# AdaLN modulation with a two-expert FFN on one core: the first unit of z with its fifth product moved forward

## The chip, the cores and the metric

The kernel runs on one core of one Trainium2 chip. The metric is the device time of one execution in microseconds, as the median of several runs. The kernel before took 1694.98 us (three runs, 1694.61 to 1696.77).

## What is computed

Cut to what matters, with x of shape (2, 2048, 512), one condition vector per batch, and all in float32:

```python
ys = y / sqrt(512)
d  = rsqrt((ys*ys) @ (weight*weight) + 1e-8)
z  = ((x * ys[:, None, :]) @ weight) * d[:, None, :]      # 4096 tokens, 512 wide
e  = argmax(softmax(z @ gate_w.T))                        # one of two experts
routed: every expert sees z where the token is its own, and zeros otherwise
        sum over experts of relu(masked @ w1[e] + b1[e]) @ w2[e] + b2[e]
shared: relu(z @ sw1 + sb1) @ sw2 + sb2
out = x + routed + shared
```

The expert that a token is not routed to sees a zero row, so that it adds a constant, `relu(b1) @ w2 + b2`.

## The kernel before, in words

The program has three parts. The first computes z from xT and the modulated weight `cws = cw * ys` (512 x 512, one for each batch), in four units of 1024 tokens, `z_unit(u)`. The second is the shared FFN over the same four units, and the third the routed FFN over tokens that are sorted by expert. Almost all of the time is in the second and third; the change touches the first unit of the first part and what is loaded for it.

Every large product is written as a 2 x 2 block product with seven block products in place of eight (Winograd's form). In `z_unit`, `a11, a12, a21, a22` are 256 x 256 blocks of `cws` (a11 and a12 are the left half of the output columns, for the low and the high rows; a21 and a22 the right half), and `x11, x12, x21, x22` are 256 x 512 blocks of xT (x11 low rows and first 512 tokens, x12 low rows and last 512, x21 and x22 the high rows). The sums of weights are `s1 = a21 + a22`, `s2 = s1 - a11`, `s3 = a11 - a21`, `s4 = a12 - s2`, and those of tokens are `x1 = x12 - x11`, `x2 = x22 - x1`, `x12 = x22 - x12` (in place) and `x4 = x21 - x2`, all on VectorE. The products are 1: a11 x11; 2: a12 x21, added onto product 1; 5: s1 x1; 6: s2 x2; 7: s3 x12; 4: a22 x4; 3: s4 x22, added onto product 5. Each is four 128 x 128 by 128 x 512 float32 matmuls, which the profile shows as eight passes (line 444).

Product 1 stays in PSUM until ScalarE has copied it (`c1`, line 459), since product 2 is added onto it. `u2 = p6 + c1` and `u3 = p7 + u2` are on VectorE (lines 469 and 476). The order on TensorE in the first unit is 1, 2, pd, 6, pv, 7, pb, 5, 4, 3. Here pd, pv and pb are the parts of a generator, `modulation_parts` (lines 229 to 261): pd multiplies `ys2 = ys * ys` by the squares of cw, which ScalarE makes; pv turns the result onto partitions, from which VectorE and ScalarE make `dd`; pb makes the bias row. `scaled` multiplies a part of z by `dd` on ScalarE (line 454). In the later units the parts of the generator are absent, and transposes of the unit before (`rows_of`, line 395) stand between the products; each is copied by ScalarE into one of four buffers with the tag `io`, scored on VectorE and stored by GpSimd.

Every engine takes its instructions in the order of the code, and a wait holds all that stands behind it on the same engine. VectorE's order in the first unit is: the four products of `modulate` for the left half, the four for the right half, the four sums of weights, ys2, rb1 (`relu(b1)`), then x1, x2, x12, x4.

PSUM has two rings of four banks, `pa` and `po`. pd, pv and pb take banks of `po`, and so do products 1 and 5; products 6, 7 and 4 take `pa`.

Transfers have three queues, issued by SyncE (SP), ScalarE (ACT) and GpSimd (POOL). The first loads are:

| Queue | Order before |
|---|---|
| SP | cond, cw left half rows 0, rows 1, rows 2 and 3 (line 146), cw right half (148), x22 (150), x for unit 1, gate |
| ACT | x11 in two parts, x21 (147), x12 (149), b1, b2 |
| POOL | 512 KB of zero rows written to zD and accD (180, 181) |

"Rows k" are the 128 rows k of cw, one k to a step of a matmul's sum. The zero rows are read much later, by gathers of padding tokens; their source is a buffer of the tag `io`, set to zero by VectorE (line 179). The transfers on SP and ACT share eight semaphores in turn, so that the ninth waits for the first to land, and so on.

Of the kernel before, what the change touches and what calls it, by code (L numbers as in the profile page):

```python
# [9 lines left out]
F32 = mybir.dt.float32  # L10
# [6 lines left out]
def kernel(  # L17
# [52 lines left out]
    U = 2 * T  # L70
# [17 lines left out]
    const = ctx.enter_context(tc.tile_pool(name="const", bufs=1))  # L88
    wpool = ctx.enter_context(tc.tile_pool(name="wpool", bufs=3))
# [18 lines left out]
    zD = dram.tile([N + P, D], F32, name="zD")  # L108
    zTD = [dram.tile([P, KD, U], F32, name=f"zTD{u}") for u in range(NU)]
    accD = dram.tile([N + P, D], F32, name="accD")  # L110
# [33 lines left out]
        nc.sync.dma_start(cw_sb[:, k, :half], cw_v[:, k, :half])  # L144
        nc.scalar.dma_start(xt[0][:, k, :T], xT_v[:, k, :T])
    nc.sync.dma_start(cw_sb[:, K2:, :half], cw_v[:, K2:, :half])
    nc.scalar.dma_start(xt[0][:, K2:, :T], xT_v[:, K2:, :T])
    nc.sync.dma_start(cw_sb[:, :, half:], cw_v[:, :, half:])
    nc.scalar.dma_start(xt[0][:, :K2, T:], xT_v[:, :K2, T:U])
    nc.sync.dma_start(xt[0][:, K2:, T:], xT_v[:, K2:, T:U])  # L150
    b1_sb = const.tile([P, E + 1, HC], F32, name="b1_sb")
    nc.scalar.dma_start(b1_sb, b1T.rearrange("e p c -> p e c"))
    b2_sb = wpool.tile([P, D], F32, tag="w1", name="b2_sb")
# [21 lines left out]
        out=before, in_=before, compare_op=ALU.is_ge, fill=1.0,  # L175
        base=0, pattern=[[-1, P]], channel_multiplier=1,
    )
    zero_rows = io("zero_rows")
    nc.vector.memset(zero_rows, 0.0)
    nc.gpsimd.dma_start(zD[N:, :], zero_rows)  # L180
    nc.gpsimd.dma_start(accD[N:, :], zero_rows)
    tok_i = const.tile([P, NB], I32, name="tok_i")
    nc.gpsimd.iota(tok_i, pattern=[[P, NB]], base=0, channel_multiplier=1)
    tok_f = const.tile([P, NB], F32, name="tok_f")
# [17 lines left out]

    ys = const.tile([P, KD, B], F32, name="ys")
    nc.vector.tensor_scalar_mul(ys, cond_sb, SCALE)
    cws = work.tile([P, B, KD, D], F32, tag="O", name="cws")

    def modulate(b, parts=(slice(0, D),)):
        for part in parts:
            for k in range(KD):
                nc.vector.tensor_scalar_mul(cws[:, b, k, part], cw_sb[:, k, part], ys[:, k, b : b + 1])  # L210
# [5 lines left out]
    def sums0(b, tile):  # L216

        sums([tile[:, i] for i in range(4)], *halves(cws[:, b]))
        return tile

    modulate(0, (slice(0, half), slice(half, D)))
    cwS = {0: sums0(0, wpool.tile([P, 4, K2, K2 * P], F32, tag="w2", name="cwS0"))}
    ys2 = const.tile([P, KD, B], F32, name="ys2")
    nc.vector.tensor_mul(ys2, ys, ys)
    cw2 = wpool.tile([P, KD, D], F32, tag="w2", name="cw2")
    dd = const.tile([P, KD, B], F32, name="dd")
    bsum = const.tile([P, KD], F32, name="bsum")
# [1 line left out]
    def modulation_parts():  # L229
        for k in range(KD):  # L230
            nc.scalar.activation(cw2[:, k, :], cw_sb[:, k, :], AF.Square)
        var = const.tile([P, KD, B], F32, name="var")
        pd = bank("po", "pd")
        for k in range(KD):
            nc.tensor.matmul(pd[:B, :D], ys2[:, k, :], cw2[:, k, :], start=(k == 0), stop=(k == KD - 1))
        vr = work.tile([P, D], F32, tag="zrow", name="vr", bufs=2)
        nc.vector.tensor_scalar_add(vr[:B, :], pd[:B, :D], EPS)
        yield
        pv = bank("po", "pv")
        for o in range(KD):  # L240
            nc.tensor.transpose(pv[:, ts(o, B)], vr[:B, ts(o, P)], ident[:B, :B])
        nc.vector.tensor_copy(var.rearrange("p k b -> p (k b)"), pv[:, : KD * B])

        root = const.tile([P, KD, B], F32, name="root")
        nc.scalar.activation(root, var, AF.Sqrt)
        d0 = const.tile([P, KD, B], F32, name="d0")
        nc.vector.reciprocal(d0, root)
        nt = const.tile([P, KD, B], F32, name="nt")
        nc.vector.tensor_mul(nt, d0, d0)
        nc.vector.tensor_mul(nt, nt, var)  # L250
        nc.vector.tensor_scalar(nt, nt, -0.5, 1.5, ALU.mult, add)
        nc.vector.tensor_mul(dd, d0, nt)
        yield

        pb = bank("po", "pb")
        for o in range(KD):
            nc.tensor.matmul(
                pb[:, o : o + 1], b2_sb[: E + 1, ts(o, P)], ones[: E + 1, :1], start=True, stop=True
            )
        nc.vector.tensor_copy(bsum, pb[:, :KD])  # L260
        yield
# [64 lines left out]

    part = {}
    rb1 = const.tile([P, E, HC], F32, name="rb1")
    nc.vector.tensor_scalar_max(rb1, b1_sb[:, :E, :], 0.0)

    zero_late = []

# [89 lines left out]
    def z_unit(u):  # L422

        b = u * U // (N // B)
        x_ = xt[u]
        z_ = zt[u] = work.tile([P, KD, U], F32, tag=f"h{2 + u % 2}", name=f"zt{u}")
        rows = list(range(U // P)) if u > 0 else []
        a11, a12, a21, a22 = halves(cws[:, b])
        s1, s2, s3, s4 = (cwS[b][:, i] for i in range(4))
        x11, x12, x21, x22 = x_[:, lo, t0], x_[:, lo, t1], x_[:, hi, t0], x_[:, hi, t1]  # L430
        x1, x2, x4 = (
            work.tile([P, K2, T], F32, tag=tag, name=f"x{i}_{u}", bufs=2)
            for i, tag in ((1, "cr"), (2, "cr"), (4, "cs"))
        )

        def product(tag, j, a, x, ps=None):
            start = ps is None
            if rows:
                rows_of(u - 1, rows.pop(0), "po" if j in (6, 7, 4, 3) else "pa")
            if start:  # L440
                ps = [bank(tag, f"z{j}_{u}_{i}") for i in range(K2)]
            for k in range(K2):
                for i in range(K2):
                    nc.tensor.matmul(
                        ps[i], a[:, k, ts(i, P)], x[:, k, :],
                        start=(start and k == 0), stop=(k == K2 - 1), skip_group_check=not start,
                    )
# [12 lines left out]
        nc.vector.tensor_sub(x1, x12, x11)  # L460
        nc.vector.tensor_sub(x2, x22, x1)
        nc.vector.tensor_sub(x12, x22, x12)
        nc.vector.tensor_sub(x4, x21, x2)
        product("po", 2, a12, x21, p1)
        if u == 0:
            next(modulation)
        p6 = product("pa", 6, s2, x2)
        for i in range(K2):
            nc.vector.tensor_add(u2[i], p6[i], c1[i])
        if u == 0:  # L470
            next(modulation)
        for i in range(K2):
            scaled(z_[:, i, t0], p1[i], i)
        p7 = product("pa", 7, s3, x12)
        for i in range(K2):
            nc.vector.tensor_add(u3[i], p7[i], u2[i])
        if u == 0:
            next(modulation)
        if u == NU - 1:
            z_sums()  # L480
            first[0][1]()
        p5 = product("po", 5, s1, x1)
        for i in range(K2):
            nc.vector.tensor_add(z_[:, K2 + i, t1], p5[i], u3[i])
            scaled(z_[:, K2 + i, t1], z_[:, K2 + i, t1], K2 + i)
        if u == 0:
            modulate(1)
        if u == NU - 1:
            first[1][1]()
        if u == 1:  # L490
            cwS[1] = sums0(1, wpool.tile([P, 4, K2, K2 * P], F32, tag="w2", name="cwS1"))
        p4 = product("pa", 4, a22, x4)
        for i in range(K2):
            nc.vector.tensor_add(z_[:, K2 + i, t0], p4[i], u3[i])
            scaled(z_[:, K2 + i, t0], z_[:, K2 + i, t0], K2 + i)
# [27 lines left out]
    for u in range(NU):  # L523
        if u == NU - 1:
            first += [made(c) for c in range(2)]
        z_unit(u)
        if u + 2 < NU:
            load_xT(u + 2)
        if u == 0:
            nc.vector.tensor_sub(gdiff, gate_sb[:, 1, :], gate_sb[:, 0, :])  # L530
        if u == 1:
            load_z(0)

# [835 lines left out]
```

## Time and profile before

| What | Value |
|---|---|
| Median of three runs | 1694.98 us (1694.61 to 1696.77) |
| The profiled execution | 1696.22 us, with a span of 1694.5 us |
| TensorE busy | 1678.6 us, 99% of the span |
| VectorE busy | 1071.9 us, 63% |
| ScalarE, GpSimd busy | 335.5 us and 221.8 us |
| Mean granted TensorE clock | 0.998 |
| DMA | 335.30 MB, a mean of 198 GB/s |
| First product starts | 6.17 us |
| First product of unit 1 starts | 42.38 us |

The span runs from the first to the last instruction of the profiled execution; its time includes what lies around them. PE is TensorE's matmuls, DVE is VectorE, ACT is ScalarE, SP is SyncE. In a timeline a line gives start, duration, engine, line of the kernel, operation, result and operands by the program's names, and in brackets how long the engine had been idle before it and what released it. In a table of stretches each engine has its busy time and its number of instructions, and the last three columns are the granted clock of TensorE, the DMA engines' busy share and GB/s.

### The profile page before, as it was taken

Reading aid. Unit: us, or ns where it says so; the run is one execution under the profiler, and the core shown is the slowest. Engines: PE = TensorE matmul, PEld = TensorE weight load, DVE = VectorE, ACT = ScalarE, POOL = GpSimd, SP = SyncE. Lnnn points to the kernel's source line nnn. Section 1 sums busy time; section 2 is a strip of 40 time slices with the busy share of each in tenths; the row PEclk is TensorE's granted clock in tenths of the full one; section 3 lists DMA queues with packets and bytes.
Section 4 is the critical chain, followed back from the end, with each engine's and each line's share of the span. In section 5 each row is a group of like instructions: output and inputs, shape, how many; then the busy total and the mean of one; then the engine's idle time right before and its main releaser. Section 6 shows DMA issues by size and latency. Waiting matters only on the chain. (4 is left out here: it accounts for less than half of the span.)

```text
span 1694.5 us, 18012 instructions
## 1 busy us (share of the span) xinstructions
PE 1678.6 (99%) x6282; PEld 1110.8 (66%) x6282; DVE 1071.9 (63%) x1749; ACT 335.5 (20%) x615; POOL 221.8 (13%) x287
## 2 busy tenths in 40 slices
PE   8999999999999999999999999999999999999998
PEld 3444478654884478645885558855588555888885
DVE  4667979888887879774872238732287322885410
ACT  2333210122002210122012220122201222013210
POOL 0212000120011200131001112002030020201210
PEclk9999999999999999999999999999999999999999
DMA  4769947597556957594734638435374353644661
GB/s 155 263 222 322 285 151 237 189 324 241 195 201 216 348 173 241 194 318 157 233 119 132 198 105 273 144 118 168 120 265 167 100 182 128 202 168 145 232 236 50
DMA packets 239744, 335.30 MB, mean 198 GB/s; under 512 B 17251, under 2 KB 175971, under 8 KB 239142
## 3 DMA queue, kind: packets, MB, share of 16 engines
q1 hardware_dynamic: 211072, 238.93, 42.4%
q0 software_dynamic: 27344, 93.61, 16.3%
q10 hardware_dynamic: 1238, 1.60, 0.3%
q8 instruction: 50, 0.82, 0.2%
q14 instruction: 40, 0.33, 0.1%
HBM read 252.55 MB, written 81.53 MB: 197 GB/s over the span
## 5 line engine op out<-in xcount | busy, mean ns | idle before, releaser
L741 PE MATMUL p1r<-zs_all,w1r 128*128 128x512 f32 (+1 forms) x256 | 106.7, 539 | 0.0
L741 PE MATMUL p5r<-zs_all,w1r 128*128 128x512 f32 (+1 forms) x256 | 106.6, 539 | 0.0
L1213 POOL DMA_INDIRECT out<-ar,idx x33 | 35.0, 1060 | 480.5 <-DVE ar L1212 429.5
L741 PE MATMUL p1s<-zs_all,w1s 128*128 128x512 f32 x192 | 91.0, 596 | 0.2 <-DVE u3s L769 0.2
L769 DVE TENSOR_TENSOR u3r<-p7r,u2r 128x512 f32<-128x512 f32 (+1 forms) x32 | 20.0, 625 | 112.5 <-PE p7r L741 111.1
L741 PE MATMUL p5s<-zs_all,w1s 128*128 128x512 f32 x192 | 90.2, 592 | 0.0
L782 DVE TENSOR_TENSOR h3r<-p5r,u2r 128x512 f32<-128x512 f32 (+1 forms) x32 | 20.0, 624 | 97.5 <-PE p5r L741 97.5
L741 PEld LDWEIGHTS p5r<-zs_all,w1r 128*128 128x128 f32 x256 | 48.6, 190 | 47.5 <-issue 45.9
L741 PEld LDWEIGHTS p1r<-zs_all,w1r 128*128 128x128 f32 x256 | 48.2, 190 | 46.0 <-issue 41.6
L741 PEld LDWEIGHTS p5s<-zs_all,w1s 128*128 128x128 f32 x192 | 36.4, 190 | 46.0 <-issue 43.3
L741 PEld LDWEIGHTS p1s<-zs_all,w1s 128*128 128x128 f32 x192 | 35.3, 190 | 38.2 <-issue 37.3
L1048 PEld LDWEIGHTS phr<-zp,ws 128*128 128x128 f32 x384 | 46.6, 192 | 11.5 <-issue 11.5
L741 PE MATMUL p7r<-zs_all,w1r 128*128 128x512 f32 (+1 forms) x128 | 53.4, 539 | 0.0
L741 PE MATMUL p6r<-zs_all,w1r 128*128 128x512 f32 (+1 forms) x128 | 53.3, 539 | 0.0
L741 PE MATMUL p4r<-zs_all,w1r 128*128 128x512 f32 (+1 forms) x128 | 53.3, 539 | 0.0
L1207 POOL DMA_INDIRECT ar<-accD,idx x33 | 34.6, 1047 | 141.1 <-PE pst L1143 129.2
L916 PE MATMUL S1s<-zs_all,w2s 128*128 128x256 f32 x224 | 52.9, 379 | 0.0
L916 PE MATMUL S2s<-zs_all,w2s 128*128 128x256 f32 x224 | 52.9, 379 | 0.0
L916 PE MATMUL a22s<-zs_all,w2s 128*128 128x256 f32 x224 | 52.9, 379 | 0.0
L418 POOL DMA_DIRECT2D zs_all<-zTD x16 | 11.5, 730 | 281.3 <-PE S1s L916 270.1
L1083 POOL DMA_DIRECT2D accD<-xr x32 | 17.8, 557 | 226.9 <-DVE xr L1082 225.1
L752 ACT ACTIVATE h3s<-h3s,b_sb 128x512 f32<-128x512 f32 x32 | 23.1, 722 | 119.5 <-DVE h3s L782 119.5
(412 smaller groups left out, 3574.4 us busy)
## 6 DMA issues: line engine op xcount, KB each, us to landing
ws<-w SPq DMA_DIRECT2D x48, 512.0 KB, 7.3
w2s<-w2S SPq DMA_DIRECT2D x28, 768.0 KB, 5.4
w1r<-s1E SPq DMA_DIRECT2D x32, 512.0 KB, 5.6
w2r<-w2E SPq DMA_DIRECT2D x21, 768.0 KB, 8.5
w1s<-s1S SPq DMA_DIRECT2D x24, 512.0 KB, 6.2
zTD<-zt POOLq DMA_DIRECT2D x8, 1024.0 KB
zD<-zr POOLq DMA_DIRECT2D x32, 256.0 KB
zs_all<-zTD POOLq DMA_DIRECT2D x16, 512.0 KB
```

Source lines behind the costliest of these rows:

```text
L418: nc.gpsimd.dma_start(zslot(slot), zTD[u][:, k : k + K2, t : t + T])
L741: nc.tensor.matmul(ps, w[:, wi + k, :], zslot(zi, W)[:, k, :], start=(start and k == 0), stop=(stop and k == K2 - 1), skip_group_check=not ...
L752: nc.scalar.activation(o, i, AF.Relu, bias=bias[:, hc : hc + 1], scale=1.0)
L769: nc.vector.tensor_add(u3, p7, u2)
L782: nc.vector.tensor_add(h12[:, c, :], p5, u2)
L916: nc.tensor.matmul(ps, w[m][:, c, :], x.of[m][:, c, :], start=(start and c == 0), stop=(c == H4 - 1), skip_group_check=not start,)
L1048: nc.tensor.matmul(ph[:, ts(i, P)], w[:, k * W + i * P : k * W + (i + 1) * P], zt[:, k, :], start=(k == 0), stop=(k == KD - 1),)
L1083: nc.gpsimd.dma_start(accD[ts(c, P), :], xr)
L1207: nc.gpsimd.indirect_dma_start(out=ar, out_offset=None, in_=accD[:, :], in_offset=at)
L1213: nc.gpsimd.indirect_dma_start(out=out[:, :], out_offset=at, in_=ar, in_offset=None)
```

## The change

In the first unit, product 5 stands right behind product 2 and ahead of pd, 6 and 7; the later units keep the old order. VectorE takes x1 first, then the right half of `modulate`, then s1, s2, s3, x2, x12, s4, x4. ys2 is made directly after ys. pd, pv and pb take banks of `pa`. Of the loads, x21 goes to POOL, the right half of cw and x22 to ACT, x12 to SP. rb1, the zeroing of the zero rows and their two writes move behind the first unit, after gdiff.

```diff
     nc.sync.dma_start(cw_sb[:, K2:, :half], cw_v[:, K2:, :half])
-    nc.scalar.dma_start(xt[0][:, K2:, :T], xT_v[:, K2:, :T])
-    nc.sync.dma_start(cw_sb[:, :, half:], cw_v[:, :, half:])
-    nc.scalar.dma_start(xt[0][:, :K2, T:], xT_v[:, :K2, T:U])
-    nc.sync.dma_start(xt[0][:, K2:, T:], xT_v[:, K2:, T:U])
+    nc.gpsimd.dma_start(xt[0][:, K2:, :T], xT_v[:, K2:, :T])
+    nc.scalar.dma_start(cw_sb[:, :, half:], cw_v[:, :, half:])
+    nc.sync.dma_start(xt[0][:, :K2, T:], xT_v[:, :K2, T:U])
+    nc.scalar.dma_start(xt[0][:, K2:, T:], xT_v[:, K2:, T:U])
...
-    zero_rows = io("zero_rows")
-    nc.vector.memset(zero_rows, 0.0)
-    nc.gpsimd.dma_start(zD[N:, :], zero_rows)
-    nc.gpsimd.dma_start(accD[N:, :], zero_rows)
...
     nc.vector.tensor_scalar_mul(ys, cond_sb, SCALE)
+    ys2 = const.tile([P, KD, B], F32, name="ys2")
+    nc.vector.tensor_mul(ys2, ys, ys)
...
-    modulate(0, (slice(0, half), slice(half, D)))
-    cwS = {0: sums0(0, wpool.tile([P, 4, K2, K2 * P], F32, tag="w2", name="cwS0"))}
-    ys2 = const.tile([P, KD, B], F32, name="ys2")
-    nc.vector.tensor_mul(ys2, ys, ys)
+    modulate(0, (slice(0, half),))
+    cwS = {0: wpool.tile([P, 4, K2, K2 * P], F32, tag="w2", name="cwS0")}
...
-        pd = bank("po", "pd")
+        pd = bank("pa", "pd")
...
-        pv = bank("po", "pv")
+        pv = bank("pa", "pv")
...
-        pb = bank("po", "pb")
+        pb = bank("pa", "pb")
...
-    nc.vector.tensor_scalar_max(rb1, b1_sb[:, :E, :], 0.0)
...
+        sub_ = nc.vector.tensor_sub
+        if u == 0:
+            sub_(x1, x12, x11)
+            modulate(0, (slice(half, D),))
+            nc.vector.tensor_add(s1, a21, a22)
+            sub_(s2, s1, a11)
+            sub_(s3, a11, a21)
+            sub_(x2, x22, x1)
+            sub_(x12, x22, x12)
+            sub_(s4, a12, s2)
+            sub_(x4, x21, x2)
+        else:
...
         product("po", 2, a12, x21, p1)
...
         if u == 0:
+            p5 = product("po", 5, s1, x1)
             next(modulation)
         p6 = product("pa", 6, s2, x2)
...
-        p5 = product("po", 5, s1, x1)
-        for i in range(K2):
-            nc.vector.tensor_add(z_[:, K2 + i, t1], p5[i], u3[i])
-            scaled(z_[:, K2 + i, t1], z_[:, K2 + i, t1], K2 + i)
+        if u > 0:
+            p5 = product("po", 5, s1, x1)
+        rest5(p5)
...
             nc.vector.tensor_sub(gdiff, gate_sb[:, 1, :], gate_sb[:, 0, :])
+            nc.vector.tensor_scalar_max(rb1, b1_sb[:, :E, :], 0.0)
+            zero_rows = io("zero_rows")
+            nc.vector.memset(zero_rows, 0.0)
+            nc.gpsimd.dma_start(zD[N:, :], zero_rows)
+            nc.gpsimd.dma_start(accD[N:, :], zero_rows)
```

`rest5` holds the two adds and the two scalings that stood behind product 5 before; in the first unit they stay behind product 7, where u3 is ready.

More of the change, by code (lines that the diff above doesn't have):

```diff
@@ L459, in z_unit, with rest1, rest5 @@
             nc.scalar.copy(c1[i], p1[i])
[L460 to L463, printed above, removed]
-        product("po", 2, a12, x21, p1)
+        sub_ = nc.vector.tensor_sub
[10 more added lines that the diff above has]
+        else:
+            sub_(x1, x12, x11)
+            sub_(x2, x22, x1)
+            sub_(x12, x22, x12)
+            sub_(x4, x21, x2)
+        product("po", 2, a12, x21, p1)
+        def rest1():
+            for i in range(K2):
+                scaled(z_[:, i, t0], p1[i], i)
+        def rest5(p5):
+            for i in range(K2):
+                nc.vector.tensor_add(z_[:, K2 + i, t1], p5[i], u3[i])
+                scaled(z_[:, K2 + i, t1], z_[:, K2 + i, t1], K2 + i)
         if u == 0:
+            p5 = product("po", 5, s1, x1)
             next(modulation)
@@ L471, in z_unit @@
             next(modulation)
-        for i in range(K2):
-            scaled(z_[:, i, t0], p1[i], i)
+        rest1()
         p7 = product("pa", 7, s3, x12)
@@ L481, in z_unit @@
             first[0][1]()
-        p5 = product("po", 5, s1, x1)
-        for i in range(K2):
-            nc.vector.tensor_add(z_[:, K2 + i, t1], p5[i], u3[i])
-            scaled(z_[:, K2 + i, t1], z_[:, K2 + i, t1], K2 + i)
+        if u > 0:
+            p5 = product("po", 5, s1, x1)
+        rest5(p5)
         if u == 0:
```

## The prediction

> **What bounds the kernel now.** The page first: TensorE is busy 99% of the span and its row of tenths has one weak slice, the first.
>
> ```profile
> span 1694.5 us, 18012 instructions
> ...
> PE 1678.6 (99%) x6282; PEld 1110.8 (66%) x6282; DVE 1071.9 (63%) x1749; ACT 335.5 (20%) x615; POOL 221.8 (13%) x287
> ...
> PE   8999999999999999999999999999999999999998
> ```
>
> So only 15.9 us are open in all, and what starts earlier on PE at the front should end earlier at the back. PE's own timeline from 5 to 24 us (start, duration, work, idle time before it and its releaser) and a table by stretches show the front:
>
> ```profile
> 6.17 1.98 PE L444 MATMUL z<-xt,cws 128*128 128x512 f32 x4 [0.89 <-DVE cws L210]
> 9.35 1.98 PE L444 MATMUL z<-xt,cws 128*128 128x512 f32 x4 [1.20 <-DVE cws L210]
> 11.71 3.67 PE L444 MATMUL z<-xt,cws 128*128 128x512 f32 x8 [0.38 <-issue]
> 17.74 5.29 PE L235 MATMUL pd<-cw,ys 128*2 128x512 f32 x8 [2.36 <-DVE rb L329]
> 22.96 1.55 PE L444 MATMUL z<-x,cwS 128*128 128x512 f32 x3
> ```
>
> ```profile
> 15.38:17.71 2.33, 0.00 (x0) 0.00 (x0) 2.30 (x7) 1.81 (x3) 0.00 (x0) 1.00 1.05 388
> 17.71:22.96 5.25, 5.22 (x8) 0.76 (x8) 4.60 (x4) 0.00 (x0) 0.00 (x0) 0.67 0.49 187
> 22.96:42.38 19.42, 19.42 (x58) 9.21 (x58) 9.84 (x22) 4.73 (x8) 0.75 (x1) 1.00 0.04 13
> ```
>
> The first two lines are product 1 (its two halves over k), the third product 2. Then PE stands still for 2.33 us, and the eight passes of pd that follow take 5.25 us: the column before the DMA share, the granted clock, is 0.67 there. The finer table has it at 0.91 from 15 to 20 us and 0.75 from 20 to 25; 9% and 25% of 5 us are together 1.7 us lost, which is one stretch of 3.4 us at half clock. From 22.96 to 42.38 nothing is open. Why pd waits is in VectorE's timeline:
>
> ```profile
> 13.72 1.14 DVE L210 TENSOR_SCALAR cws<-cw_sb,ys 128x256 f32<-128x256 f32 x4 [1.85 <-DMA cw_sb<-cw]
> 14.90 0.69 DVE L196 TENSOR_TENSOR cwS<-cws 128x512 f32<-128x512 f32 x1
> 15.62 0.69 DVE L197 TENSOR_TENSOR cwS<-cwS,cws 128x512 f32<-128x512 f32 x1
> 16.23 0.68 DVE L198 TENSOR_TENSOR cwS<-cws 128x512 f32<-128x512 f32 x1
> 16.84 0.68 DVE L199 TENSOR_TENSOR cwS<-cws,cwS 128x512 f32<-128x512 f32 x1
> 17.44 0.16 DVE L224 TENSOR_TENSOR ys<-ys 128x8 f32<-128x8 f32 x1
> 17.51 0.17 DVE L329 TENSOR_SCALAR rb<-b_sb 128x32 f32<-128x32 f32 x1
> 17.60 1.22 DVE L460 TENSOR_TENSOR x<-xt 128x1024 f32<-128x1024 f32 x1
> ```
>
> pd needs ys2 (L224), a 0.16 us instruction that stands behind the right half's four products and four sums. The profile names the neighbouring rb (L329), since the wait on VectorE ends there. Product 6, next in PE's order, needs s2 and x2 (ready at 20.1), so without pd's wait it would itself have waited.
>
> **What the Trainium skill says.** "TensorE: Matmul & The Clock Gate", Part 1 (The HAM clock gate): the clock is halved after a little-used window of about 3.4 us, and the windows run free of the program. The trace agrees: 0.5 for 3.4 us after the idle stretch. It follows that another execution may lose that window or not. "DMA: Bandwidth & Descriptors", Queues, rings and completion order (Arbitration): the DMA engines turn round-robin between queues, packet by packet. The trace agrees: the 4 KB cond (32-byte pieces, SP's queue) landed at 4.1 us, as late as the 256 KB beside it on ACT's. Same page, Issuing engines are not separate DMA queues: a third queue brings no bandwidth. So what counts below is the order of bytes.
>
> **The change part by part.**
> *Loads.* The trace's landing events, before: cw rows 0 at 5.7, rows 1 at 8.9, rows 2-3 at 11.2, right half at 13.7 (all SP); x blocks x11 at 5.5, x21 at 9.5, x12 at 12.3 (ACT), x22 at 15.1 (SP). The zero rows' writes (512 KB, POOL) lay among them, 6.8 to 10.6. The change takes those 512 KB away and puts x21, also 512 KB, on POOL's queue. All first loads together are 3.08 MB, and what product 5 needs is 2.56 MB. No bandwidth is gained; 0.5 MB at the 377 GB/s of 6.17 to 15.38 is 1.4 us of other traffic fewer. In turns of one packet per queue and DMA engine (1 KB for half rows of cw, 2 KB for x), rows 2-3 of cw were through after some 45 turns at 10.5 us with 2.58 MB moved; now 45 turns hold 2.16 MB, so about 1.1 us earlier, landing near 10.2. Rows 1 come perhaps 0.5 us earlier (8.4), the right half at about 11, x12 at about 11.8, x22 at about 13.5. x12 comes no earlier in turns, being last on SP; 12.3, as now, is its upper value, a good 11 the lower. POOL's first transfer before was issued at 1.88 and its first packet moved at 6.8, 4.9 us later, against 1.1 to 1.4 in later quiet stretches. Issued at about 0.8, x21 begins between 2.1 and 6.8; I take 5.7, and with 16 turns of 0.2 us and the slowest engine it lands near 9.7 (bounds 7.5 and 12). On POOL it stands ahead of ident and the iotas, but two issues of 0.75 and 0.58 us leave: tok_i is not later. Each hardware transfer after the first eight waits for the landing eight before it:
>
> ```profile
> SPq L136 <- DMA cw_sb<-cw: 6.3, 2, 4.4
> ...
> SPq L150 <- DMA cond_sb<-condT: 0.8, 1, 0.8
> ```
>
> With x21 gone from that row, x1's load for unit 1 goes out at about 5.5 instead of 8.93; it lies behind x12 on SP, and shares with x22 alone, which has 3 us to spare.
> *ys2, rb1, zero memset.* ys2 costs 0.16 us at about 4.4, where VectorE waits for cw anyway. The three at the end of unit 0 add 0.17 + 0.48 us on VectorE at 43.4 (before), where it stood 0.67 us idle for ACT: nothing.
> *Order.* Product 2: left half of cw at 10.2 + 0.62 us of scaling, and ACT's copies of p1 (0.59 each), which end 0.6 us after product 1. Product 1 ends at 8.4 + 0.4 + 1.98 = 10.8, so product 2 starts at about 11.2 and ends at 14.9 (before 11.71 and 15.38). Product 5: x12 at 11.8, x1 1.22, four scalings 1.14, s1 0.69, hand-overs 0.15: ready at 15.0. Product 5 (3.6) to 18.6; pd follows at full clock, 8 x 0.43 = 3.45 us, to 22.1. Its squares on ACT (2.2 us) are done by 14, ys2 long before. VectorE goes on with s2 15.7, s3 16.3, x2 17.5, x12 18.6, s4 19.3, x4 20.5: all ahead of products 6, 7, 4. Product 6 starts at 22.1 instead of 22.96, and product 5 (3.55 us of PE between 31.54 and 35.07) is gone behind it. Gain 0.86 + 3.55 = 4.4 us: 2.7 by open time (2.33 and 0.4 from earlier loads), 1.7 by clock. Product 4 now follows product 7 and pb directly; x4 is 10 us old. Product 3 adds onto p5's banks after VectorE has read them: u3, bsum, two adds, some 2.8 us after product 7, against 4.7 us of pb and product 4. The scaling for the second batch (1.67) then delays product 4's adds by 1.7 us; the transposes that read them come 3.6 us later. Free.
> *Banks.* pd, pv and pb move to the other four: each predecessor there (idle, p6, p7) is read before its turn comes. Nothing.
> *Zero rows.* Two issues on POOL (0.75, 0.58) after unit 0's second store. That store was issued at 43.89 and landed at 54.4; the rows' stores behind it landed at 55.0, 55.9 and 56.7, 256 KB per 0.9 us. The zero writes come between and land at about 56. Their buffer is the one that ACT's fourth copy of rows in unit 1 fills (54.19 before): that copy waits 1.9 us, VectorE's score behind it too, and u3's add (56.77) 0.8 us. Cover: the banks of product 7 are asked for again only in product 4, after 61. Nothing, up to a landing at some 58.
>
> **Sum.** The profiled execution took 1696.22 us, 1.7 more than its span: 1696.22 - 4.4 = 1691.8. It lies 1.24 above the median, 1694.98 (runs 1694.61, 1694.98, 1696.77). If that is the profiler's own, the changed kernel takes 1694.98 - 4.4 = 1690.6; if it is the lost window, which the changed kernel has in no execution, 1691.8. I take **1691.2**.
>
> **Rivals.** (a) *x12 or x21 late.* For: the 4.9 us of POOL's first transfer, x12 last on SP. Against: 0.5 MB less traffic. From x12 at 13.3 on, product 5 starts at 16.5, and 1.5 us of the gain go: 1692.7. (b) *Gain taken back later.* PE has later waits (1.20 us at 130.96, 1.28 at 288.40); the first is released by ACT's copy behind PE's own work and moves along, so I find no fixed date. It would give 1695: the change then doesn't do what it says. (c) *Loads much better*: cw rows 1 before 8.1, no gap inside product 1, product 5 at 14.0 or PE started before 6.17: one us more, 1689.8. (d) *Slower: the zero rows stall unit 1.* They stand behind 2 MB of stores on a queue that took 10.5 us for one of these. From a landing at 58 on, each us goes onto PE; slower than before by 0.2% needs 4.4 + 3.4 us, a landing near 66. That would be 1698.5. Against: queue shares do not change there, only 0.5 MB more.
>
> **Chances and range.** About 0.2% (3.4 us) is what a measurement of this kernel tells from no change. Main case 0.70, its times 1690 to 1692.3 round 1691.2; 0.46 of it lies under 1691.6, the bound. (c) 0.10, faster. (a) 0.10 and (b) 0.04, the same. (d) 0.06, slower. Faster 0.56, same 0.38, slower 0.06. Range 1689.2 to 1694.0: it takes in (c) and (a) and x21's bounds, with a run's scatter of some 0.4 below; the main case alone is 1690.2 to 1692.3.
>
> **What would show it.** Right: product 5 follows product 2 on PE with under 1 us open, at 14.5 to 15.5; pd 3.5 us at clock 1.00; product 6 near 22; unit 1's first product near 38. x21 landed by 11 or product 2 waits for it. ACT's fourth copy in unit 1 some 2 us late with no open PE. Wrong: a wait on x12 or x21 of over 1 us, a half-clock stretch after 6 us, or a new PE gap between 38 and 130.

## The result, and the profile after

The changed kernel takes 1692.99 us (median of 22 runs, 1692.11 to 1694.25) against 1694.97 us before (22 runs, 1694.26 to 1696.91). The ratio is 0.9986, with a 95% interval of 0.998 to 0.9993. So it is faster by 2.0 us, and by less than the 0.2% that the prediction took as its bound. The times of the kernel before lie in two groups, 15 of the 22 from 1694.3 to 1695.5 and 7 from 1696.5 to 1696.9, while those of the changed kernel lie in one.

The profiled execution of the changed kernel took 1692.93 us with a span of 1691.2 us. Its page:

```profile
span 1691.2 us, 18009 instructions
...
PE 1678.5 (99%) x6282; PEld 1111.1 (66%) x6282; DVE 1071.1 (63%) x1749; ACT 335.2 (20%) x615; POOL 221.8 (13%) x288
```

The span is 3.3 us shorter. TensorE's busy time is what it was (1678.6) only by chance: pd is 1.7 us shorter, but in this execution full clock was first granted at 9.45 us, in place of 5.40 before, so that the first half of product 1 ran at half clock and took about 1.7 us more. The clock column reads 1.00 there too, since it counts only what follows the first grant; but the passes of product 1 start 0.85 us apart up to 9.4 and 0.43 after it, and its weight loads show it as well:

```profile
7.69 0.34 PEld L439 LDWEIGHTS z<-xt,cws 128*128 128x128 f32 x1 [0.52 <-issue]
10.29 0.19 PEld L439 LDWEIGHTS z<-xt,cws 128*128 128x128 f32 x1 [0.24 <-issue]
```

TensorE's timeline at the front of the changed kernel, one merged line for products 1 and 2, then products 5, pd and 6:

```profile
5.82 9.00 PE L439 MATMUL z<-xt,cws 128*128 128x512 f32 x16 [0.54 <-DVE cws L208]
15.90 3.70 PE L439 MATMUL z<-x,cwS 128*128 128x512 f32 x8 [1.07 <-DVE cwS L460]
19.53 3.60 PE L231 MATMUL pd<-cw,ys 128*2 128x512 f32 x8
23.05 3.70 PE L439 MATMUL z<-x,cwS 128*128 128x512 f32 x8
```

The same as a table of stretches of the changed kernel (busy time of PE, PEld, DVE, ACT, POOL, then granted clock, DMA share, GB/s):

```profile
14.82:15.90 1.08, 0.01 (x2) 0.01 (x1) 1.01 (x4) 0.49 (x1) 0.00 (x0) 1.00 1.05 389
15.90:19.53 3.63, 3.63 (x9) 1.44 (x10) 3.63 (x5) 0.00 (x0) 0.00 (x0) 1.00 0.67 254
19.53:23.05 3.52, 3.52 (x9) 0.59 (x8) 1.65 (x2) 0.00 (x0) 0.00 (x0) 1.00 0.00 0
23.05:39.04 15.99, 15.99 (x50) 7.69 (x50) 9.55 (x22) 4.62 (x8) 0.78 (x1) 1.00 0.04 15
```

The wait of 2.33 us is now one of 1.08 us, pd takes 3.52 us in place of 5.25 because the clock stayed at 1.00, and nothing is open from there to the first product of unit 1, at 39.04 in place of 42.38. The shift is kept to the end: from the first transpose of unit 1 (41.94 before, 38.60 after) to TensorE's last matmul it is 1646.5 us in both traces. Over all traces but that of zeros_x4 below this stretch takes 1646.5 to 1647.5 us, so that single executions differ by up to 1 us behind the front.

What is left of the wait is in VectorE's timeline of the changed kernel:

```profile
10.10 0.61 DVE L208 TENSOR_SCALAR cws<-cw_sb,ys 128x256 f32<-128x256 f32 x2 [0.98 <-DMA cw_sb<-cw]
12.84 1.22 DVE L458 TENSOR_TENSOR x<-xt 128x1024 f32<-128x1024 f32 x1 [2.12 <-DMA xt<-xT]
13.98 1.13 DVE L208 TENSOR_SCALAR cws<-cw_sb,ys 128x256 f32<-128x256 f32 x4
15.15 0.69 DVE L460 TENSOR_TENSOR cwS<-cws 128x512 f32<-128x512 f32 x1
```

VectorE stands idle for 2.12 us until x12 lands (12.71 by the landing events) and only then takes up the right half of cw, which had landed at 10.35. Product 5 waits for s1 at the end of that row.

### The profile page after: what moved, and what is told of

It reads as the page before. It is cut to its first block, busy times and chain, and to the rows that moved or that the text cites. A ratio compares the mean times of both kernels' runs of the same rounds, so it can differ in the third digit from the quotient of the medians.

```text
span 1691.2 us, 18009 instructions
## 1 busy us (share of the span) xinstructions
PE 1678.5 (99%) x6282; PEld 1111.1 (66%) x6282; DVE 1071.1 (63%) x1749; ACT 335.2 (20%) x615; POOL 221.8 (13%) x288
## 5 line engine op out<-in xcount | busy, mean ns | idle before, releaser
L938 PE MATMUL S1s<-zs_all,w2s 128*128 128x256 f32 x224 | 52.9, 379 | 0.0
L938 PE MATMUL S2s<-zs_all,w2s 128*128 128x256 f32 x224 | 52.9, 379 | 0.0
L938 PE MATMUL a22s<-zs_all,w2s 128*128 128x256 f32 x224 | 52.9, 379 | 0.0
```

The source lines that it names most:

```text
L938: nc.tensor.matmul(ps, w[m][:, c, :], x.of[m][:, c, :], start=(start and c == 0), stop=(c == H4 - 1), skip_group_check=not start,)
```

## The experiments

The open questions after the result were three. Which part earns the gain: the new order with the moved product (the prediction's theory), or the loads? What makes the last 1.08 us? And are the two groups of times before the lost clock window? The kernel before was timed beside each of them on the same chip; the share of its upper group differs from chip to chip, and its median with it (1694.85 to 1695.99), so that small differences are best read from the ratios.

| Kernel | Median us (runs) | Ratio to before, 95% |
|---|---|---|
| changed | 1692.99 (22) | 0.9986 [0.998, 0.9993] |
| order_only | 1692.92 (16) | 0.9985 [0.9977, 0.9992] |
| loads_only | 1692.65 (14) | 0.998 [0.9972, 0.9988] |
| ys2_only | 1693.45 (21) | 0.9989 [0.9983, 0.9996] |
| weights_first | 1691.53 (8) | 0.9976 [0.9965, 0.9986] |
| filled | 1694.44 (13) | 0.9993 [0.9985, 1.0002] |
| zeros_front | 1695.26 (13) | 0.9996 [0.9988, 1.0005] |
| zeros_x4 | 1699.27 (9) | 1.0026 [1.0016, 1.0036] |
| weights_warm | 1691.99 (12) | 0.9977 [0.9968, 0.9985] |
| two_queues | 1693.03 (21) | 0.999 [0.9983, 0.9996] |
| zeros_late | 1693.88 (21) | 0.9991 [0.9985, 0.9998] |
| after_again | 1692.98 (21) | 0.9985 [0.9979, 0.9992] |

### One part at a time

**order_only**: the changed kernel with this part taken back.

```diff
-    nc.gpsimd.dma_start(xt[0][:, K2:, :T], xT_v[:, K2:, :T])
-    nc.scalar.dma_start(cw_sb[:, :, half:], cw_v[:, :, half:])
-    nc.sync.dma_start(xt[0][:, :K2, T:], xT_v[:, :K2, T:U])
-    nc.scalar.dma_start(xt[0][:, K2:, T:], xT_v[:, K2:, T:U])
+    nc.scalar.dma_start(xt[0][:, K2:, :T], xT_v[:, K2:, :T])
+    nc.sync.dma_start(cw_sb[:, :, half:], cw_v[:, :, half:])
+    nc.scalar.dma_start(xt[0][:, :K2, T:], xT_v[:, :K2, T:U])
+    nc.sync.dma_start(xt[0][:, K2:, T:], xT_v[:, K2:, T:U])
...
+    zero_rows = io("zero_rows")
+    nc.vector.memset(zero_rows, 0.0)
+    nc.gpsimd.dma_start(zD[N:, :], zero_rows)
+    nc.gpsimd.dma_start(accD[N:, :], zero_rows)
     tok_i = const.tile([P, NB], I32, name="tok_i")
...
-            zero_rows = io("zero_rows")
-            nc.vector.memset(zero_rows, 0.0)
-            nc.gpsimd.dma_start(zD[N:, :], zero_rows)
-            nc.gpsimd.dma_start(accD[N:, :], zero_rows)
```

> The order of the change alone: loads, their queues and the zero rows stay as in the kernel before; product 5 ahead of pd, x1 ahead of the right half on VectorE, ys2 early. With the loads of before, x12 lands at 12.3 and the right half of cw at 13.7, so s1 is ready at 13.72 + 1.14 + 0.69 = 15.6, product 5 starts at 15.65, pd at 19.2, product 6 at 22.7. The kernel before, with no half-clock stretch, would have product 6 at 21.2 and product 5 (3.55) still to come, 24.75 in all: a gain of 2.0 us on the lower group of its times (about 1694.6), so 1692.6. Order theory (the moved product earns the gain): 1692.6, as good as the whole change. Loads theory (the re-ordered loads earn it): 1694.6 or no lower than 1694.

Measured: 1692.92 us, the whole change's time. TensorE's timeline of order_only, products 1 and 2, then 5, pd and 6:

```profile
6.27 9.21 PE L443 MATMUL z<-xt,cws 128*128 128x512 f32 x16 [0.99 <-DVE cws L212]
15.32 3.62 PE L443 MATMUL z<-x,cwS 128*128 128x512 f32 x8
18.87 3.60 PE L235 MATMUL pd<-cw,ys 128*2 128x512 f32 x8
22.40 3.70 PE L443 MATMUL z<-x,cwS 128*128 128x512 f32 x8
```

Product 5 follows product 2 with nothing open, at 15.32, no later than in the whole change (15.90, and 15.36 in after_again below), although the zero rows' 512 KB are still among the first loads. The order alone, with ys2's early place in it, is worth the whole gain, and the two changes to the loads add nothing to it.

**loads_only**: the loads' lines of the change and the late zero rows and rb1, in the kernel before.

```diff
-    nc.scalar.dma_start(xt[0][:, K2:, :T], xT_v[:, K2:, :T])
-    nc.sync.dma_start(cw_sb[:, :, half:], cw_v[:, :, half:])
-    nc.scalar.dma_start(xt[0][:, :K2, T:], xT_v[:, :K2, T:U])
-    nc.sync.dma_start(xt[0][:, K2:, T:], xT_v[:, K2:, T:U])
+    nc.gpsimd.dma_start(xt[0][:, K2:, :T], xT_v[:, K2:, :T])
+    nc.scalar.dma_start(cw_sb[:, :, half:], cw_v[:, :, half:])
+    nc.sync.dma_start(xt[0][:, :K2, T:], xT_v[:, :K2, T:U])
+    nc.scalar.dma_start(xt[0][:, K2:, T:], xT_v[:, K2:, T:U])
...
             nc.vector.tensor_sub(gdiff, gate_sb[:, 1, :], gate_sb[:, 0, :])
+            nc.vector.tensor_scalar_max(rb1, b1_sb[:, :E, :], 0.0)
+            zero_rows = io("zero_rows")
...
```

> The loads of the change alone, with the zero rows and rb1 put behind the first unit; the order on TensorE and VectorE stays as before, product 5 last but two. Order theory: pd or product 6 still waits for VectorE, so that only the 0.4 to 0.6 us of earlier loads are gained: 1694.1. Loads theory: the right half of cw landed at 10.35 in the changed kernel's trace, so VectorE makes right half and sums by 14.6, ys2 by 14.7, x2 by 17.1; product 2 ends at 14.8, pd runs 14.9 to 18.4, product 6 starts at 18.4. With product 5 still to come that is 21.95 against 24.75: 2.8 us, 1691.8, which is 1.1 us better than the whole change, whose product 5 waits for x1.

Measured: 1692.65 us. VectorE and TensorE in loads_only:

```profile
10.29 1.67 DVE L206 TENSOR_SCALAR cws<-cw_sb,ys 128x256 f32<-128x256 f32 x6 [1.55 <-DMA cw_sb<-cw]
11.99 0.69 DVE L192 TENSOR_TENSOR cwS<-cws 128x512 f32<-128x512 f32 x1
...
14.53 0.16 DVE L220 TENSOR_TENSOR ys<-ys 128x8 f32<-128x8 f32 x1
```

```profile
6.57 8.68 PE L439 MATMUL z<-xt,cws 128*128 128x512 f32 x16 [1.28 <-DVE cws L206]
15.18 3.60 PE L231 MATMUL pd<-cw,ys 128*2 128x512 f32 x8
18.70 3.70 PE L439 MATMUL z<-x,cwS 128*128 128x512 f32 x8
```

In the old order VectorE goes straight from the left half to the right half (one row of six), ys2 is made at 14.53, and pd stands right behind product 2. The wait is gone without moving product 5. Of the 2.8 us expected about 2 came: in this trace product 1 started at 6.57, 0.4 us later than before, and ran at half clock until 9.54. ScalarE's copy of its first half therefore ended at 11.49, and product 2 began at 11.56, though its weights were scaled by 10.9; it ended at 15.2 in place of 14.8. The start of product 1 varies from execution to execution (5.6 to 6.6); in every trace it follows the landing of rows 0 of cw (5.2 to 6.1) by 0.4 to 0.5 us. What sets that landing was not tried.

**ys2_only**: in the kernel before, one line moved.

```diff
     nc.vector.tensor_scalar_mul(ys, cond_sb, SCALE)
+    ys2 = const.tile([P, KD, B], F32, name="ys2")
+    nc.vector.tensor_mul(ys2, ys, ys)
...
-    ys2 = const.tile([P, KD, B], F32, name="ys2")
-    nc.vector.tensor_mul(ys2, ys, ys)
```

> One instruction of the change alone: ys2 right after ys in the kernel before. Theory that pd's wait of 2.33 us hangs on ys2 alone: pd starts at 15.4, behind product 2; the wait then passes to product 6, whose x2 is ready at 20.0, so product 6 starts at 20.1 against 21.2 without the half clock: 1.1 us on the lower group, 1693.5. No gap is then over 1.4 us, so no half-clock stretch and no upper group of times. Rival (pd waits for ScalarE's squares or a PSUM bank as well): pd stays near 17.7 and the time at 1694.6.

Measured: 1693.45 us, as worked out. In its timeline pd comes forward to 14.97, and the wait passes to product 6, which stands 1.26 us for x2:

```profile
14.97 3.60 PE L235 MATMUL pd<-cw,ys 128*2 128x512 f32 x8
19.82 3.70 PE L444 MATMUL z<-x,cwS 128*128 128x512 f32 x8 [1.26 <-DVE x L461]
```

The forecast that no upper group would be left did not hold, though it lies lower than before: 14 of the 21 times lie from 1692.8 to 1693.7 and 7 from 1694.1 to 1695.3. The profiled execution (1694.08) is one of the seven and has no half-clock stretch at the front; it lost 1.0 us behind the first transpose of unit 1 (1647.5 us in place of 1646.5). What makes these seven was not tried.

**zeros_late**: in the kernel before, the zero rows alone behind the first unit.

```diff
-    zero_rows = io("zero_rows")
-    nc.vector.memset(zero_rows, 0.0)
-    nc.gpsimd.dma_start(zD[N:, :], zero_rows)
-    nc.gpsimd.dma_start(accD[N:, :], zero_rows)
...
             nc.vector.tensor_sub(gdiff, gate_sb[:, 1, :], gate_sb[:, 0, :])
+            zero_rows = io("zero_rows")
+            nc.vector.memset(zero_rows, 0.0)
+            nc.gpsimd.dma_start(zD[N:, :], zero_rows)
+            nc.gpsimd.dma_start(accD[N:, :], zero_rows)
```

> The kernel before with its zero rows alone put behind the first unit; queues, order, ys2 and rb1 as before. The right half lands near 12.2 in place of 13.3 to 13.7; right half and sums of VectorE end at 15.9, ys2 and rb1 at 16.1, pd starts at 16.1 and product 6 at 19.6 at full clock (x2 ready at 18.6). Against 21.2 that is 1.6 us: 1693.0 and no second group of times, the wait being 1.5 us at most. Rival (the zero rows cost nothing at the front): 1694.6 with a second group above 1696.

Measured: 1693.88 us, a smaller gain than expected, and the wait of 1.5 us at most did not come. The loads did come earlier (right half 11.45, rows 2-3 of cw 8.61), but product 2 came earlier with them, so that the wait stayed:

```profile
15.50 5.29 PE L231 MATMUL pd<-cw,ys 128*2 128x512 f32 x8 [2.16 <-DVE rb L325]
```

pd starts 2.24 us earlier than before and is again at half clock. Four parts, each by itself, brought 0.09% to 0.20%, and all together 0.14%, with intervals that overlap: the traces show them working on the same wait, and it can be taken away once.

### What makes the last microsecond

**weights_first**: the changed kernel with two steps exchanged.

```diff
-            sub_(x1, x12, x11)
             modulate(0, (slice(half, D),))
             nc.vector.tensor_add(s1, a21, a22)
+            sub_(x1, x12, x11)
```

> The changed kernel with two steps exchanged on VectorE: right half of cw and s1 ahead of x1. In its trace VectorE stood idle from 10.7 to 12.84 for x12 while the right half had landed at 10.35, and product 5 started 1.07 us after product 2. Theory that VectorE's order makes this wait: right half 10.7 to 11.9, s1 12.6, x1 12.84 to 14.1, so product 5 follows product 2 at 14.8 and the time falls by 1.05 us, to 1691.9. Rival (the landing of x12 alone sets it, or another wait stands right behind it): 1692.9 as now.

Measured: 1691.53 us. VectorE and TensorE in weights_first:

```profile
9.63 1.67 DVE L208 TENSOR_SCALAR cws<-cw_sb,ys 128x256 f32<-128x256 f32 x6 [1.19 <-DMA cw_sb<-cw]
11.33 0.69 DVE L459 TENSOR_TENSOR cwS<-cws 128x512 f32<-128x512 f32 x1
12.32 1.23 DVE L460 TENSOR_TENSOR x<-xt 128x1024 f32<-128x1024 f32 x1 [0.30 <-DMA xt<-xT]
```

```profile
8.50 5.50 PE L439 MATMUL z<-xt,cws 128*128 128x512 f32 x12 [0.79 <-DVE cws L208]
13.84 3.60 PE L439 MATMUL z<-x,cwS 128*128 128x512 f32 x8
17.36 3.60 PE L231 MATMUL pd<-cw,ys 128*2 128x512 f32 x8
```

The 1.8 us of weights are done while x12 is under way, x1 is the last step, and product 5 follows product 2 without a gap. The order is worth the 1.08 us of the changed kernel's wait; that product 5 starts 2.1 us earlier in this trace (13.84 against 15.90) is also because full clock came at 5.88, and rows 1 of cw at 8.1 in place of 8.7, so that product 2 was over earlier. This kernel has the lowest median here. It and the changed kernel were timed on different chips, and their intervals against the kernel before overlap a little.

**weights_warm**: weights_first with eleven warm-up matmuls at the start in place of nine.

```diff
-    for _ in range(9):
+    for _ in range(11):
         nc.tensor.matmul(idle[:, :P], ones, ones, start=True, stop=True)
```

> weights_first with eleven in place of nine warm-up matmuls at the start, so that TensorE is busy without a break to about 6.2 us. In the profiled executions so far full clock was granted at 4.5, 5.4, 5.9, or only at 9.4, 9.5, 10.3 us; in the late ones product 1 runs at half clock. Theory that a break of 0.5 to 1.3 us ahead of product 1 costs a whole clock window: full clock by 7.9 us in every execution, product 2 ends near 14.0, median 1691.1 and a narrower spread than 1690.9 to 1692.7. Rival (product 1 is bound by cw's landing, not by the clock): 1691.5, no change.

Measured: 1691.99 us, and the ratio is that of weights_first, so no gain is shown, as the rival had it. In its trace full clock was granted at 4.4 us, and product 5 still started at 13.84, as in weights_first: rows 1 of cw (landed at 8.0 and 8.1) set product 1's second half. But weights_first's own trace had full clock at 5.9, so that the pair of traces doesn't show what a late grant costs in this order.

**zeros_front**: the changed kernel, zero rows and their writes back at the front.

```diff
+    zero_rows = io("zero_rows")
+    nc.vector.memset(zero_rows, 0.0)
+    nc.gpsimd.dma_start(zD[N:, :], zero_rows)
+    nc.gpsimd.dma_start(accD[N:, :], zero_rows)
     tok_i = const.tile([P, NB], I32, name="tok_i")
...
-            zero_rows = io("zero_rows")
-            nc.vector.memset(zero_rows, 0.0)
-            nc.gpsimd.dma_start(zD[N:, :], zero_rows)
-            nc.gpsimd.dma_start(accD[N:, :], zero_rows)
```

> The changed kernel with the zeroing of the zero rows and their two writes put back to the front, behind the load of x21 on POOL. Loads theory (512 KB fewer among the first loads are 1.4 us): the writes share the DMA engines with cw rows 2-3, the right half and x12, which land 0.7 to 1.4 us later; product 5 starts near 17.0 in place of 15.9 and the time is 1694.0. Rival (order alone counts, since order_only with those writes at the front was as fast as the whole change): 1693.0.

Measured: 1695.26 us, worse than expected, and no better than before. Its VectorE:

```profile
11.76 0.62 DVE L212 TENSOR_SCALAR cws<-cw_sb,ys 128x256 f32<-128x256 f32 x2 [2.51 <-DMA cw_sb<-cw]
14.27 1.23 DVE L462 TENSOR_TENSOR x<-xt 128x1024 f32<-128x1024 f32 x1 [1.89 <-DMA xt<-xT]
```

and the same step in order_only:

```profile
11.72 1.23 DVE L462 TENSOR_TENSOR x<-xt 128x1024 f32<-128x1024 f32 x1 [0.35 <-DMA xt<-xT]
```

zeros_front and order_only move the same bytes at the front and differ only in the queues. x12 lands at 14.1 on the new ones and at 11.7 on the old ones (11.7 to 12.3 in the four traces that have the old queues and the zero rows at the front). So with the zero rows at the front the new queues make x12 late by 1.8 to 2.4 us, and the zero rows' removal (to between 12.1 and 12.7, in the six traces of the changed loads) pays back most of it.

**two_queues**: the changed kernel with the old loads' lines (the first eight lines of order_only's diff), zero rows left behind.

> The changed kernel with the loads back on the queues of the kernel before (x21 and x12 on ACT, right half of cw and x22 on SP, nothing of them on POOL); zero rows and rb1 stay behind the first unit, and the order of the change stays. With the zero rows at the front the old queues landed x12 at 11.7 and the right half at 13.3 (order_only), the new ones 14.1 and 11.9 (zeros_front), and the times were 1692.9 and 1695.3. Queue theory (the new queues make x12 late by themselves, and the zero rows' removal only pays that back): without the zero rows the right half lands near 12.2, s1 is ready near 14.1, product 5 follows product 2 without a gap at about 14.5, and the time is 1691.9. Rival (512 KB fewer bring nothing with the old queues): 1692.9, like order_only.

Measured: 1693.03 us. The expected mechanism failed: the right half came far earlier than forecast (10.1 in place of 12.2), but x12 no earlier than in order_only, and product 5 waits for it. VectorE and TensorE in two_queues:

```profile
7.89 0.61 DVE L208 TENSOR_SCALAR cws<-cw_sb,ys 128x256 f32<-128x256 f32 x2 [0.81 <-DMA cw_sb<-cw]
11.93 1.22 DVE L458 TENSOR_TENSOR x<-xt 128x1024 f32<-128x1024 f32 x1 [3.42 <-DMA xt<-xT]
```

```profile
5.65 7.22 PE L439 MATMUL z<-xt,cws 128*128 128x512 f32 x16 [0.36 <-DVE cws L208]
14.98 5.40 PE L439 MATMUL z<-x,cwS 128*128 128x512 f32 x8 [2.12 <-DVE cwS L460]
```

x12 lands at 11.9, 0.8 us earlier than in the changed kernel, and product 5 starts 0.9 us earlier. But with x21 and cw at 7.1 and 7.9 product 2 is over at 12.9, the wait grows to 2.12 us, and in this execution a clock window is lost, so that product 5 takes 5.40 us. Eight of its 21 times lie at 1694.3 or above, the others from 1692.0 to 1693.5. In the changed kernel, two_queues and zeros_front product 5 starts 3.1 to 3.2 us after x12's landing (12.71, 11.90 and 14.14; starts 15.90, 14.98 and 17.32): x1, the right half and s1 in a row, as VectorE's order has them.

**after_again**: the changed kernel beside the two before.

> The changed kernel itself beside the two others on the same chip: 1693.0, with product 5 some 0.8 to 1.1 us behind product 2.

Measured: 1692.98 us. The wait of product 5 is longer than expected:

```profile
15.36 3.70 PE L439 MATMUL z<-x,cwS 128*128 128x512 f32 x8 [1.41 <-DVE cwS L460]
```

Though it waits longer than in the first trace (1.07), product 5 starts 0.5 us earlier (15.36 against 15.90). Full clock came at 4.98 here and product 2 was over at 13.95, while x12 landed at 12.17 in place of 12.71. So the length of this wait alone doesn't tell what it costs.

### The clock

**filled**: the kernel before with idle matmuls in the wait.

```diff
         product("po", 2, a12, x21, p1)
         if u == 0:
+            for _ in range(9):
+                nc.tensor.matmul(idle[:, :P], ones, ones, start=True, stop=True)
             next(modulation)
```

> The kernel before with nine further small matmuls (128 x 128, their result unused) on TensorE between product 2 and pd, about 2.1 us at full clock, so that the wait of 2.33 us is filled with idle work. Clock theory: the second group of times of the kernel before (1696 and above, about 2 us over the first) is the executions in which the wait falls into one clock window and is followed by 3.4 us at half clock. Filled, pd still starts near 17.7 but runs 3.5 us at full clock in every execution: median 1694.7, none above 1695.8. Rival (the second group comes from something else): a third or more of the times stays above 1696.

Measured: 1694.44 us. TensorE in filled:

```profile
14.84 2.17 PE L467 MATMUL idle<-ones 128*128 128x128 f32 x18
17.34 3.59 PE L235 MATMUL pd<-cw,ys 128*2 128x512 f32 x8 [0.32 <-DVE rb L329]
```

pd starts about where it did and takes 3.59 us. One of 13 times lies over 1695.8 (1696.26), against 18 of 36 of the kernel before on the same chip. The granted clock of the single executions agrees. It is on record for the 141 executions of the kernel before that were timed beside the experiments: of the 80 under 1695.7 us, 37 show a mean clock of 1.000 to three digits, and of the 54 from 1696 on none does (means 0.9995 and 0.9987; one stretch of 3.41 us at half clock is 0.0010 of 1694 us). So the upper group is the lost window, up to that one execution of filled, which stays unexplained. Over all traces the window was lost where TensorE's wait was 2.1 us or more (kernel before, two_queues, zeros_late), and not where it was 1.44 us or less.

Why a wait of 2.33 us costs a window in some executions only can be worked out from the 13 traces. The half-clock stretches at the front last 3.413 us. Cut each trace into stretches of this length, counted from its first grant of full clock, and take TensorE's busy share of each (by the profile's modelled ends of the matmuls). The three windows lost at the front follow stretches that are 37 or 38% busy; after the last matmuls full clock ends behind a stretch of 40% or less; and it was kept behind all the others, some 6,400, of which the least busy has 47%. So a wait costs a window when enough of it falls into one stretch, and where the stretches lie differs from execution to execution. That the busy share decides is read from these traces and was not tried by itself.

### The cover of the zero rows

In the changed kernel the two late writes landed at 51.9 and 52.9 us. ScalarE's timeline, with its fourth copy of unit 1 into their buffer:

```profile
53.05 0.59 ACT L396 COPY zr<-pt 128x512 f32<-128x512 f32 x1 [4.32 <-DMA accD<-zero_rows]
```

In the kernel before that copy stood at 54.19, which is 50.85 after the shift of 3.34 us; so it is 2.2 us late. TensorE has no gap there. **zeros_x4** makes the two writes four times.

```diff
-            nc.gpsimd.dma_start(zD[N:, :], zero_rows)
-            nc.gpsimd.dma_start(accD[N:, :], zero_rows)
+            for _ in range(4):
+                nc.gpsimd.dma_start(zD[N:, :], zero_rows)
+                nc.gpsimd.dma_start(accD[N:, :], zero_rows)
```

> The changed kernel with the two zero-row writes behind the first unit made four times over, so 1.5 MB more on POOL's queue. It tests the cover that the prediction gave them (no cost up to a landing at 58 of the kernel before, which is 54.7 here). In the changed kernel they landed at 51.9 and 52.9 and ScalarE's fourth copy came 2.2 us late with no gap on TensorE. Six more at 0.95 us each land at 58.6; the fourth copy, the score and u3 follow, and u3's first half is done near 60.6, when product 4's second bank is due at 58.9: a gap of 1.7 us or more in unit 1, and 1694.7 to 1696. Rival (the writes are hidden however many they are): 1693.0.

Measured: 1699.27 us, worse than expected. ScalarE and TensorE in zeros_x4:

```profile
60.96 1.27 ACT L396 COPY zr<-pt 128x512 f32<-128x512 f32 x2 [12.27 <-DMA accD<-zero_rows]
```

```profile
58.35 1.02 PE L439 MATMUL z<-x,cws 128*128 128x512 f32 x2
62.28 2.84 PE L439 MATMUL z<-x,cws 128*128 128x512 f32 x6 [2.90 <-ACT zr L396]
```

The last write landed at 60.7, the copy followed at 60.96, and product 4 of unit 1 stopped before its second bank, in the place that the prediction's rival (d) and its cover name. The first product of the shared FFN is then 4.7 us later against unit 1's start than in the changed kernel (88.8 us against 84.2). The rest of the loss of 6.3 us lies later and was not followed. The expectation had the last landing at 58.6 and a gap of 1.7 us. The place was right and the cover larger than said: a landing at 52.9 cost nothing, and one 7.8 us later cost 4.7 us, where the prediction's "each us goes onto PE" from 54.7 (its 58, less the shift) on would have made 6.0.

## Why the prediction was right or wrong

*Direction and range* held: faster, and 1692.99 lies in 1689.2 to 1694.0. The main case (1690 to 1692.3, given 0.70) did not come, and neither did the likeliest class, faster by over 0.2% at 0.56: 2.0 us of the 3.8 forecast were measured, which falls under "same", given 0.38. The time lies nearest to that of rival (a), 1692.7, given 0.10; the range held because it took that rival in. Two of the three signs of being wrong came: TensorE stood 1.08 us for x12, where "over 1 us" was the sign, and there was a half-clock stretch after 6 us, that of product 1 up to 9.45. The second cost nothing in this execution, since product 5 stood waiting for x12 anyway; it had not been foreseen. Product 5 (15.90, where 14.5 to 15.5 was to show the prediction right), product 6 and unit 1's first product each came about 1 us after the time forecast.

*The wait and its releaser* were right. ys2_only moves one 0.16 us instruction and gains what was worked out, and the wait goes to product 6 and x2 as said. pd at full clock (3.45 forecast, 3.52 measured), no new gap before unit 1 and none that the change made after, product 4 and product 3 without a wait, the banks: right.

*The loads* were right but for one. Rows 2-3 of cw landed at 10.1 (10.2 forecast), rows 1 at 8.7 (8.4), the right half at 10.4 (11), x22 at 13.1 (13.5), x21 at 8.5 (9.7, its first packet 3.5 us after its issue). The third queue brought no bandwidth, as forecast: from 6 to 12 us the engines moved 372 GB/s, and 373 before. Product 2 ended at 14.8 (14.9), which is in part luck: the half clock in product 1 had not been counted, and it held product 2 (11.14) behind ScalarE's copy of product 1, its weights being ready at 10.7.

**The term that was mis-sized first: x12's landing.** The step "x12 at about 11.8", with "12.3, as now, is its upper value", failed: it landed at 12.7, and product 5 started at 15.9 in place of 15.0. That makes 0.9 of the 1.1 us between the sum against the profiled execution's own time (1691.8) and the changed kernel's profiled time (1692.93). Over the six traces with these loads x12 landed at 12.1 to 12.7, so that 0.9 is the upper end, and 0.3 the lower. The upper value had no ground: x12 came to stand last on SP behind three pieces of half rows, and order_only against zeros_front shows the queues alone making it about 2 us later while the zero rows are at the front. The turns were also counted with pieces of 2 KB for x21, while in the traces POOL moves it in 128 packets of 4 KB: from 6 to 8 us of the changed kernel POOL moved 348 KB, and SP and ACT, whose pieces were then 1 KB, 187 and 184 KB. What share of the delay this makes was not tried. As a step: the old landing was taken as a bound for a transfer that had been moved to another queue.

**The second: the clock's 1.7 us on the median.** The sum counted them in full and left open only whether the profile's 1.24 us over the median were the profiler's. They were the lost window, as its trace has it: the profiled execution of before, at 1696.22, lies by the upper group, and 15 of 22 executions have no such window to win back. From the lower group (about 1694.6) the gain is 1.6 us, from the upper one 3.8. The prediction had it from the Trainium skill ("TensorE: Matmul & The Clock Gate", Part 1) that windows run free, which filled and the two groups bear out, and wrote that "another execution may lose that window or not". It then took the middle between the sum from the profiled time (1691.8), which contains the loss, and one from the median (1690.6), which takes the loss from a number that doesn't contain it.

*Rivals.* (a), x12 late, is what happened in part: 12.7 where it asked for 13.3. (b), a gain taken back later, is not seen: 1646.5 us in both traces, and in the others 1646.9 to 1647.5 with the zero rows at the front and 1647.0 to 1647.3 with them behind. (c) did not come. (d) has its place and its mechanism shown by zeros_x4, and no cost at the change's own size.

*What the prediction did not ask*: whether the parts are worth their price by themselves. Moving product 5 and re-ordering the loads are two ways of taking away one wait.

## What to carry to other kernels

Cost the parts of a change one by one against the same wait: those that remove it do not add up, and here one moved 0.16 us instruction had over half of the effect of all of them (0.11% of 0.14%, by ratios whose intervals overlap). In a chain of vector work that feeds the next product, put the step whose operand lands last at the end, and what is already there ahead of it (weights_first: the wait of 1.08 us was gone). Before a stretch at half clock is counted as gain, look at how many of the timed executions contain it.

## What was not expected of the hardware

A transfer's place in the queues can count for as much as 0.5 MB of traffic. With the zero rows at the front, x12 landed at 14.1 behind half rows of cw (1 KB pieces) on SP, and at 11.7 to 12.3 behind x21 (2 KB pieces) on ACT, with the same bytes; without the zero rows the difference is only 0.2 to 1.0 us (12.1 to 12.7 against 11.7 and 11.9). Taking the 0.5 MB away brought x12 forward by 1.4 to 2.0 us on the new queues, and by 0.7 us at most on the old ones. The size of the pieces enters, as the prediction's turns of one packet per queue have it: from 9 to 10 us of order_only SP and ACT moved about as many packets (117 and 125), which were 119 KB on SP, in pieces of 1 KB, and 256 KB on ACT, in pieces of 2 KB. How much of x12's delay comes from this, and how much from what stands ahead of it in its queue, was not tried.

Where full clock was first granted differed from trace to trace with the same warm-up matmuls: at 4.5, 4.8, 5.0, 5.4, 5.6, 5.6, 5.9 and 6.5 us, and at 9.4, 9.5, 9.9 and 10.3 us in others. In the late ones the first half of product 1 runs at half clock. In the changed kernel's trace this cost nothing, in that of loads_only up to 0.6 us, by an estimate from its trace (product 2 at 11.56 with its weights scaled by 10.9). The stretches of 3.413 us tell the two kinds apart: the one that ends with the grant is 87 to 100% busy in all 13 traces, and the one before it is 71 to 84% busy in the four late ones, where the pause between the warm-up matmuls (over by 5.28) and product 1 falls into it. This too was not tried by itself.
